# Output norm of three samples and one sample's token scales on ScalarE, four statistics ahead of the branch, half of the last residuals on VectorE

## The chip, the cores and the metric

The kernel runs on one NeuronCore of a Trainium2 chip, in one launch. A core has a matrix engine (TensorE; PE in the profile, PEld for its weight loads), a vector engine (VectorE, DVE), an engine for functions of one operand with a scale and a bias (ScalarE, ACT), a general engine (GpSimd, POOL) and a queue engine that issues transfers (SyncE, SP). Each runs its own instructions in the order in which the program lists them, and waits on semaphores for the others. PE writes to PSUM, which has 8 banks of 128 x 512 numbers; all else lies in SBUF or in HBM. The metric is the device time of one execution in microseconds. Everything is computed in 32-bit floats.

## The reference

Two layers work on x of 16 samples, 256 channels and 64 x 64 pixels (4096 tokens a sample). The first is linear attention with 4 heads of 32, the second a mixture of two out of four convolution experts:

```python
# layer 0
xn  = rmsnorm(gn(x))                       # gn: 32 groups of 8 channels; rmsnorm over channels, per token
q, k, v = split(w_qkv @ xn)                # 3 x 128 rows
q = softmax(q, over the 32 of a head); k = softmax(k, over tokens)
context = k @ v^T                          # per head, 32 x 32
out = w_out @ (context^T @ (q * 32**-0.5)) + b_out
x   = x + rmsnorm(out) * g_out             # rmsnorm over channels, per token
# layer 1
y   = gn(x)
prob = softmax((mean over pixels of y) @ router_w.T / 2); best 2 of 4, weights normalised
for the two experts i of a sample:
    h = gelu(depthwise3x3_i(y) + dw_b_i)
    x = x + weight_i * (pw_i @ h + pw_b_i)
```

## The kernel before

**Tiling.** Channels are the partitions, in two halves of 128 (index k or m). A sample's tokens form 8 groups of 512 (index g) and, for the experts, 4 quarters of 1024 (index j). One sample's x is kept in SBUF in four buffers ("ring") from the first sum to the store, and three samples are under way at once in different phases.

**Phases of a sample.** The names in brackets are functions of the program and tiles of the profile.

1. "in": x is loaded (`load_a`, xa) and BNStats on DVE gathers its statistics (`stats`, st, 16 a sample, one for each g and k; line 264); the `gn0_` functions make a scale and a bias for each channel, with two small PE matmuls (pg, pd). For sample 0 the statistics read the ring directly.
2. "q": x is loaded again (`load_b`, xb); `norm` applies scale and bias (xg, 2 a group: line 305 on DVE for samples below the constant EARLY, line 307 on ACT for the others). PE transposes xg (`turn_x`, px); ACT squares and sums each token (`x_squares`, jx); `token_scale` makes 1/rms (r: a DVE instruction, line 241, and a power on POOL, line 242); `x_keep` writes the scaled tokens (xt, 4 a group: line 331 on DVE below EARLY, line 333 on ACT else). PE projects xg to q and k (`project`, pq); ACT takes the exponential with that scale (`evacuate`, e); PE sums the context over all groups in one bank (`context`, pc); q's softmax follows (`q_sum` on DVE, `q_norm` on POOL, `q_turn` on PE, `q_keep` on ACT). At the end the `mix_` functions fold context, v's weight and the output weight into one matrix (mw).
3. "out": PE applies it (`attend`, po, two halves hf a group); ACT squares and sums (`out_squares`, junk); `out_scale` makes 1/rms (s, DVE and POOL); `out_norm` multiplies (ob: line 463, one DVE instruction of 128 x 512 a half; for the last sample line 461, two ACT instructions of 128 x 256); PE transposes back (`out_turn`, tr); DVE adds to x in the ring (`out_add`, line 477); ACT gathers square sums for the second group norm (`square_sums`).
4. "route": the second norm's scale and bias, the router, the two experts and their weights.
5. "x", by quarters. The depthwise convolution of the first channel half is done on PE: ACT writes a padded copy (`pad0`, pd), SP lays it out in HBM (`lay`) and reads it back spread over partitions (`spread`, xr, 8 a quarter), PE multiplies it by band matrices (`conv0`, dw), ACT applies gelu in place (`gelu0`, line 727). The second half is done on DVE: `pad1` and `start1` on ACT, then 8 taps for each expert (`tap1`, acc, line 741, 128 x 1024), gelu on ACT (`gelu1`, h, line 750). The pointwise matmuls (`pointwise`) collect a quarter in four banks: two parts from h (line 768, weights picked by DVE, lines 591 and 593), two parts from xr with 32-row matmuls (line 779, psp). `residual` adds the bank, the bias and x in one DVE instruction (line 795, 8 a quarter). For the last sample PE adds x by a fifth part, an identity matmul (line 774, 16 records a quarter), and ACT adds the bias only (line 793). `store` writes the result.

**Order.** Every step is a row (phase, sample, group or quarter, name). `place()` gives each row a time: the start of its phase for this sample, plus the slot of the phase times the group, plus the row's own offset from the table PLAN. Rows are sorted by it and issued under a manual schedule, so that this table alone fixes the order on every engine and queue. The unit is a 64th of a sample's period. The first samples and the last have shorter slots for some phases (`in_first`, `q_first`, `out_first` and so on) and shifted starts (`x_0`, `q_1`, `out_e1` and so on; `e1` is the last sample, `e2` the one before).

**Head.** `block_kernel` loads sample 0's x into the ring (16 transfers), then the projection weight; DVE scales the weight (line 1494) and squares it (line 1502), PE sums the columns (pn, line 1505), DVE takes the maximum and compares (lines 1507 and 1508), the result is read into registers (line 1509), and a branch (line 1510) chooses the pipelined path or a general one. The pipelined path's first instructions build small constants on DVE (lines 157 to 174) among the first statistics.

Of the kernel before, what the change touches and what calls it, by code (L numbers as in the profile page):

```python
# [10 lines left out]
FP = mybir.dt.float32  # L11
# [5 lines left out]
P = 128  # L17
# [30 lines left out]
EARLY = 3  # L48
# [5 lines left out]
    "load_x1": 2.47, "mean": 1.04, "means": 4.69, "dev": 5.07, "devs": 8.24, "scale": 8.52,  # L54
# [4 lines left out]
    "evacuate3": 6.83, "context": 7.87, "q_sum": 8.01, "q_norm": 13.4, "q_turn": 15.77,  # L59
    "q_keep": 16.04, "mix_a": 8.41, "mix_turn": 9.67, "mix_v": 10.33, "mix_vv": 11.49, "mix_b": 12,  # L60
    "mix_out": 12.87, "mix_c": 13.33, "mix_lead": 15.68, "attend0": -0.16, "out_sq0": 0.33,
# [3 lines left out]
    "means1": 7.77, "scale1": 8.7, "router": 9.48, "route": 9.99, "choose": 12.08,  # L65
    "pick_taps": 16.41, "route_lead": 22.29, "pick_rows0": 12.27, "pick_rows1": 15.38,
    "pick_row_bias": 13.7, "weigh": 19.29, "pick_bias": 20.19, "pick000": 1.5, "pick100": 11.76,
# [17 lines left out]
    "in_first": 2.74, "in_more": 1.74, "q_first": 9.11, "out_first": 7.86, "out_more": 15.48,  # L85
# [1465 lines left out]
```

## Time and profile before

| | |
|---|---|
| runs | 2724.4 us median of 4 (2722.22 to 2725.16) |
| the profiled execution | 2722.04 us; span 2720.3 us; granted PE clock 0.992 |
| busy: PE, DVE, ACT, POOL | 2635.9 (97%), 2417.5 (89%), 2083.3 (77%), 767.5 us (28%) |
| taps, line 741 (DVE) | 1304.7 us, 1024 of 1284 ns |
| residuals, line 795 (DVE) | 214.5 us, 480 of 475 ns |
| output norm, line 463 (DVE) | 163.6 us, 240 of 682 ns |
| norm, line 307 (ACT) | 169.4 us, 208 of 814 ns |
| token scales, line 333 (ACT) | 168.5 us, 416 of 485 ns |
| identity matmuls, line 774 (PE) | 16.4 us, 64 records |
| moved between HBM and SBUF | 394.77 MB, mean 145 GB/s |

The mean ns of a group are from start to end of one instruction; instructions in a row overlap a little, so that busy time divided by the count is less. The profile has stages with different limits: up to 97 us sample 0 fills the pipeline alone, to 317 us samples 1 and 2 join, to 2425 us all samples look alike, and the last 300 us empty it. The shares over the whole span hide these stages.

### The profile page before, as it was taken

The page shows a single profiled execution, that of the slowest core. Times are in us where ns is not written, and L with a number is a line of the kernel's source. Part 1 is how long each engine was busy: PE and PEld are TensorE (multiplying, and loading weights), DVE is VectorE, ACT ScalarE, POOL GpSimd, SP SyncE. Part 2 cuts the span into 40 slices and gives each one's busy share as a digit, 9 for nine tenths or more (in the row PEclk, how much of TensorE's full clock was granted, in tenths as well). Part 3 has the DMA queues.
Part 4 walks back from the last instruction along what each step waited for, and adds up shares of the span by engine and source line. Part 5 has one row for each costly group of instructions (what it writes and reads, how often), then busy time and mean ns, then how long its engine had stood idle before and what let it go on. Part 6 is the DMA issues. An engine that isn't in the chain of part 4 may idle for free.

```text
span 2720.3 us, 55294 instructions
## 1 busy us (share of the span) xinstructions
PE 2635.9 (97%) x19300; PEld 2257.0 (83%) x19300; DVE 2417.5 (89%) x4480; ACT 2083.3 (77%) x5230; POOL 767.5 (28%) x874
## 2 busy tenths in 40 slices
PE   6898999999999999999999999999999999998888
PEld 5787888888888888888888888888888888886767
DVE  6889998999989898898989989898898988889994
ACT  3576788887887888788787888888788788876643
POOL 2342232322323222232322323233222323232200
PEclk9999999999999999999999999999999999999989
DMA  4335454464545446355354545445454443524332
GB/s 156 113 124 149 140 171 153 133 166 155 155 146 159 156 146 185 128 162 171 126 169 153 156 154 158 155 144 173 142 160 154 145 135 122 149 86 133 122 113 89
DMA packets 229711, 394.77 MB, mean 145 GB/s; under 512 B 25904, under 2 KB 108336, under 8 KB 229424
## 3 DMA queue, kind: packets, MB, share of 16 engines
q1 hardware_dynamic: 228880, 390.75, 46.6%
q8 instruction: 156, 2.56, 0.4%
q14 instruction: 131, 1.07, 0.1%
q10 hardware_dynamic: 544, 0.39, 0.0%
HBM read 280.82 MB, written 110.23 MB: 144 GB/s over the span
## 4 chain that ended last, share of the span: by engine, by line
PE 88%; DVE 7%; ACT 2%; issue 1%; POOL 1%; DMA 1%; ACTq 0%; DVEq 0%; POOLq 0%
PE pw L779 17%; PE pw L768 16%; PE dw L719 15%; PE pq L346 14%; PE pc L364 8%; PE po L440 8%; PE px L315 4%; PE tr L468 4%; DVE acc L741 3%; PE ptq L387 2%; DVE st L264 1%; PE pw L774 1%; DVE ring L795 1%; DVE ring L477 0%; DMA xr<-lay 0%
## 5 line engine op out<-in xcount | busy, mean ns | idle before, releaser
L741 DVE SCALAR_TENSOR_TENSOR acc<-pd,ds,acc 128x1024 f32<-128x1024 f32 x1024 | 1304.7, 1284 | 14.0 <-ACT acc L734 10.2
L242 POOL TENSOR_TENSOR s<-s,mhalf 128x2 f32<-128x2 f32 x256 | 212.3, 831 | 1104.8 <-DVE s L241 1087.0
L346 PE MATMUL pq<-wqkv_n,xg 128*128 128x256 f32 x2048 | 503.9, 384 | 0.9
L719 PE MATMUL dw<-xr,taps 128*128 128x256 f32 x2048 | 489.2, 381 | 8.6 <-ACT xr L727 6.7
L768 PE MATMUL pw<-h,pw 128*128 128x256 f32 x2048 | 481.6, 384 | 15.7 <-ACT h L750 10.0
L779 PE MATMUL pw<-xr,psp 32*128 32x256 f32 x8192 | 484.1, 382 | 0.0
L779 PEld LDWEIGHTS pw<-xr,psp 32*128 32x128 f32 x8192 | 405.3, 185 | 66.2 <-issue 47.2
L768 PEld LDWEIGHTS pw<-h,pw 128*128 128x128 f32 x2048 | 383.0, 192 | 74.8 <-ACT h L750 12.4
L719 PEld LDWEIGHTS dw<-xr,taps 128*128 128x128 f32 x2048 | 374.5, 190 | 59.1 <-ACT xr L727 11.8
L346 PEld LDWEIGHTS pq<-wqkv_n,xg 128*128 128x128 f32 x2048 | 370.2, 191 | 57.8 <-ACT xt L333 11.7
L322 ACT ACTIVATE jx<-px 128x256 f32<-128x256 f32 x512 | 195.4, 382 | 193.5 <-PE px L315 174.4
L354 ACT ACTIVATE e<-pq,r 128x256 f32<-128x256 f32 x512 | 219.7, 470 | 133.8 <-PE pq L346 118.2
L242 POOL TENSOR_TENSOR r<-r,mhalf 128x4 f32<-128x4 f32 x128 | 186.1, 1454 | 448.6 <-DVE r L241 425.3
L795 DVE SCALAR_TENSOR_TENSOR ring<-pw,bs,ring 128x256 f32<-128x256 f32 x480 | 214.5, 475 | 65.7 <-PE pw L768 37.2
L440 PE MATMUL po<-mw,qt 128*128 128x256 f32 x1024 | 253.1, 381 | 0.7 <-DVE ring L795 0.7
L727 ACT ACTIVATE xr<-dw,bv 128x256 f32<-128x256 f32 x512 | 219.5, 478 | 39.7 <-PE dw L719 37.7
L364 PE MATMUL pc<-xt,e 128*128 128x257 f32 x1024 | 245.8, 382 | 3.4 <-DVE xt L331 3.2
L484 ACT ACTIVATE sqj<-ring,nm 128x512 f32<-128x512 f32 x256 | 185.8, 726 | 71.3 <-DVE ring L477 69.5
L477 DVE SCALAR_TENSOR_TENSOR ring<-tr,gout,ring 128x512 f32<-128x512 f32 x256 | 188.8, 746 | 41.5 <-PE tr L468 36.0
L448 ACT ACTIVATE junk<-po 128x256 f32<-128x256 f32 x512 | 196.3, 383 | 27.1 <-PE po L440 22.3
L364 PEld LDWEIGHTS pc<-xt,e 128*128 128x128 f32 x1024 | 189.4, 191 | 29.2 <-issue 2.9
L440 PEld LDWEIGHTS po<-mw,qt 128*128 128x128 f32 x1024 | 190.2, 190 | 28.0 <-issue 2.0
(144 smaller groups left out, 3570.1 us busy)
## 6 DMA issues: line engine op xcount, KB each, us to landing
xr<-lay SPq DMA_DIRECT2D x1024, 66.0 KB
ring<-in_x SPq DMA_DIRECT2D x256, 256.0 KB
out<-ring SPq DMA_DIRECT2D x128, 512.0 KB
xa<-in_x SPq DMA_DIRECT2D x240, 256.0 KB
xb<-in_x SPq DMA_DIRECT2D x240, 256.0 KB
lay<-pd SPq DMA_DIRECT2D x64, 594.0 KB
psp<-layp SPq DMA_DIRECT2D x128, 128.0 KB
layp<-pw SPq DMA_DIRECT2D x16, 256.0 KB
```

What stands on the lines that cost most here:

```text
L242: nc.gpsimd.tensor_tensor(out_t, out_t, mhalf[:, :n], ALU.pow)
L346: nc.tensor.matmul(pq, xg[:, k, c * P : (c + 1) * P], wqkv[:, k, : 2 * HID], start=(k == 0), stop=(k == KH - 1),)
L354: nc.scalar.activation(live["e", b, g][:, c], live["pq", b, g, c // 2][:, c % 2], AF.Exp, scale=live["r", b, g][:, c : c + 1],)
L364: nc.tensor.matmul(live["pc", b], live["e", b, g][:, c, HID:], xt[g % 2][:, c], start=(g == 0 and c == 0), stop=(g == NG - 1 and c == CG - 1),
L440: nc.tensor.matmul(po[:, c], qt[:, n * P : (n + 1) * P], live["mw", b], start=True, stop=True)
L448: nc.scalar.activation(junk[:, :C], live["po", b, g, hf][:, c], AF.Square, accum_out=ss[:, c : c + 1])
L719: nc.tensor.matmul(po, live[f"taps{g}", b][:, d * P : (d + 1) * P], rows3[:, :, d : d + W // 2], start=(d == 0), stop=(d == 1),)
L727: nc.scalar.activation(live["xr", b, j, g][:, 0 : GT // 2], po, AF.Gelu, bias=live["bv", b][:, g : g + 1])
L741: nc.vector.scalar_tensor_tensor(acc, pd1[j % 2][:, t // 3 : t // 3 + QR, t % 3 : t % 3 + W], live["ds", b][:, i, t : t + 1], acc, ALU.mul ...
L768: nc.tensor.matmul(po[q], live["pw1", b][:, part, ms], h[:, q % 2, q // 2], start=begin, stop=end,)
L779: nc.tensor.matmul(po[q], live["psp", b][band, g, ms], live["xr", b, j, g][band, 0 : GT // 2], start=begin and g % 4 == 0, stop=end and g ...
L795: nc.vector.scalar_tensor_tensor(xo, po, bs, xo, ALU.add, ALU.add)
```

## The change

It has five parts. EARLY goes from 3 to 2, so that sample 2's 16 norms and 32 token scales are done by ACT instead of DVE. `out_norm` of samples 0 and 1 is done by ACT, as that of the last sample was already: 64 more ACT instructions of 128 x 256, and 32 fewer on DVE of 128 x 512. Four statistics of sample 0 (groups 0 and 1) are issued in the head, ahead of the branch, into a tile of the head's pool (`st_0`); the other statistics tiles have one buffer instead of two. In the last sample, only quarters 0 and 1 add x by identity matmuls; for quarters 2 and 3 `residual` on DVE adds bank, bias and x, and 32 PE records fall away. And the order: every offset of PLAN has a new value, the depthwise steps of the second channel half (`pad1`, `start1`, `tap1`, `gelu1`) form a phase of their own, "v", and the last sample has its own slots for "x" (15.66 instead of 16) and "v" (15.52), with a shift of the start of "v" (0.34).

```diff
-EARLY = 3
+EARLY = 2
+HEAD_STATS = 2
 PLAN = {
-    "load_x1": 2.47, "mean": 1.04, "means": 4.69, "dev": 5.07, "devs": 8.24, "scale": 8.52,
+    "load_x1": 4.91, "mean": 0.71, "means": 2.85, "dev": 3.38, "devs": 7.33, "scale": 7.4,
...
-    "evacuate3": 6.83, "context": 7.87, "q_sum": 8.01, "q_norm": 13.4, "q_turn": 15.77,
+    "evacuate3": 6.7, "context": 9.31, "q_sum": 9.23, "q_norm": 11.69, "q_turn": 15.93,
...
+    "in_e1": 0.05, "in_e2": 0.12, "pw04": 19.61, "pw14": 23.04, "x_last": 15.66, "v_last": 15.52,
+    "v_e1": 0.34,
 }
...
+    live["st", 0] = st_0
     def stats(b, g, k):
-        st = live["st", b] if ("st", b) in live else new(small, [P, KH, NG, 6], "st", b, bufs=2)
+        st = live["st", b] if ("st", b) in live else new(small, [P, KH, NG, 6], "st", b, bufs=1)
...
-        if b == NB - 1:
+        if b in (0, 1, NB - 1):
             for c in range(2):
                 nc.scalar.activation(ob[:, c], po[:, c], AF.Copy, scale=s[:, c : c + 1])
...
-        n = 5 if b == NB - 1 else 4
+        n = 5 if by_pe(b, j) else 4
...
+    def by_pe(b, j):
+        return b == NB - 1 and j < NQ // 2
...
-        if b == NB - 1:
+        if by_pe(b, j):
             nc.scalar.activation(xo, po, AF.Identity, bias=bs)
...
-                at("in", b, g, f"stats{k}", stats, b, g, k)
+                if b or g >= HEAD_STATS:
+                    at("in", b, g, f"stats{k}", stats, b, g, k)
...
-            at("x", b, j, "pad1", pad1, b, j)
+            at("v", b, j, "pad1", pad1, b, j)
             for i in range(TOPK):
-                at("x", b, j, f"start{i}", start1, b, j, i)
+                at("v", b, j, f"start{i}", start1, b, j, i)
                 for t in range(1, 9):
-                    at("x", b, j, f"tap{i}{t}", tap1, b, j, i, t)
-                at("x", b, j, f"gelu1{i}", gelu1, b, j, i)
+                    at("v", b, j, f"tap{i}{t}", tap1, b, j, i, t)
+                at("v", b, j, f"gelu1{i}", gelu1, b, j, i)
...
-                for part in range(5 if b == NB - 1 else 4):
+                for part in range(5 if by_pe(b, j) else 4):
...
-            "out": turn[0], "route": SLOT, "x": 2 * SLOT,
+            "out": turn[0], "route": SLOT, "x": 2 * SLOT, "v": 2 * SLOT,
         }
-        start = {"x": PERIOD * b}
+        if b == NB - 1:
+            slot |= {"x": PLAN["x_last"], "v": PLAN["v_last"]}
+        start = {"x": PERIOD * b, "v": PERIOD * b}
...
+    st_0 = head.tile([P, KH, NG, 6], FP, name="st_0")
...
         nc.vector.tensor_tensor(sq, wqkv[:, :, : 2 * HID], wqkv[:, :, : 2 * HID], ALU.mult)
+        for g in range(HEAD_STATS):
+            for k in range(KH):
+                nc.vector.bn_stats(st_0[:, k, g], ring[g // 2][:, k, g % 2])
```

More of the change, by code (lines that the diff above doesn't have):

```diff
@@ L53, with pipelined_path @@
 PLAN = {
-    "load_x1": 2.47, "mean": 1.04, "means": 4.69, "dev": 5.07, "devs": 8.24, "scale": 8.52,
[4 rows of a table removed]
-    "evacuate3": 6.83, "context": 7.87, "q_sum": 8.01, "q_norm": 13.4, "q_turn": 15.77,
-    "q_keep": 16.04, "mix_a": 8.41, "mix_turn": 9.67, "mix_v": 10.33, "mix_vv": 11.49, "mix_b": 12,
-    "mix_out": 12.87, "mix_c": 13.33, "mix_lead": 15.68, "attend0": -0.16, "out_sq0": 0.33,
[3 rows of a table removed]
-    "means1": 7.77, "scale1": 8.7, "router": 9.48, "route": 9.99, "choose": 12.08,
-    "pick_taps": 16.41, "route_lead": 22.29, "pick_rows0": 12.27, "pick_rows1": 15.38,
-    "pick_row_bias": 13.7, "weigh": 19.29, "pick_bias": 20.19, "pick000": 1.5, "pick100": 11.76,
[17 rows of a table removed]
-    "in_first": 2.74, "in_more": 1.74, "q_first": 9.11, "out_first": 7.86, "out_more": 15.48,
[12 rows of a table removed]
+    "load_x1": 4.91, "mean": 0.71, "means": 2.85, "dev": 3.38, "devs": 7.33, "scale": 7.4,
[4 rows of a table added]
+    "evacuate3": 6.7, "context": 9.31, "q_sum": 9.23, "q_norm": 11.69, "q_turn": 15.93,
+    "q_keep": 16.06, "mix_a": 10.35, "mix_turn": 11.12, "mix_v": 11.38, "mix_vv": 11.77,
+    "mix_b": 12.09, "mix_out": 13.34, "mix_c": 13.4, "mix_lead": 15.68, "attend0": 0.19,
[5 rows of a table added]
+    "pick_row_bias": 13.88, "weigh": 18.75, "pick_bias": 19.18, "pick000": 1.16, "pick100": 11.36,
[17 rows of a table added]
+    "in_first": 2.73, "in_more": 1.58, "q_first": 9.08, "out_first": 18.07, "out_more": 12.28,
[13 rows of a table added]
 }
 @with_exitstack
-def pipelined_path(ctx, tc, ring, wqkv, x, w_outT, b_out, g_out, router_wT, router_b, dw, dw_b, pwT, pw_b, out):
+def pipelined_path(ctx, tc, ring, st_0, wqkv, x, w_outT, b_out, g_out, router_wT, router_b, dw, dw_b, pwT, pw_b, out):
     nc = tc.nc
@@ L908, in pipelined_path @@
         for phase in start if near else ():
-            start[phase] += PLAN[f"{phase}_{near}"]
+            start[phase] += PLAN[f"{phase}_{near}"] if phase != "v" or near == "e1" else 0
         starts[b], slots[b] = start, slot
@@ L913, in place @@
         phase, b, g, key = row[:4]
-        pace = 1 if phase in ("route", "x") else slots[b][phase] / SLOT
+        pace = 1 if phase in ("route", "x", "v") else slots[b][phase] / SLOT
         return starts[b][phase] + slots[b][phase] * g + PLAN[key] * pace
@@ L1510, in block_kernel @@
     with tc.If(small_logits > 0) as branch:
-        pipelined_path(tc, ring, wqkv, x, *weights_and_out)
+        pipelined_path(tc, ring, st_0, wqkv, x, *weights_and_out)
     with branch.Else():
```

73 rows, old and new, of the table PLAN are left out of this document.

## The prediction

> **What bounds the kernel now.** I read the whole span first as a table of stretches, cut where the stage changes (columns: stretch and its length, then busy time of PE, PEld, DVE, ACT, POOL, granted PE clock, DMA share, GB/s).
>
> ```profile
> 0.00:97.00 97.00, 63.25 (x310) 51.68 (x310) 68.06 (x181) 34.16 (x108) 25.00 (x43) 0.96 0.41 135
> 97.00:174.00 77.00, 76.58 (x438) 68.15 (x437) 66.26 (x173) 58.96 (x203) 30.25 (x35) 1.00 0.38 127
> 174.00:317.00 143.00, 129.66 (x838) 109.70 (x837) 136.96 (x278) 98.46 (x265) 44.57 (x51) 0.95 0.50 148
> 317.00:479.00 162.00, 161.92 (x1203) 139.63 (x1202) 147.27 (x272) 133.87 (x333) 46.99 (x53) 1.00 0.50 155
> ...
> 2425.00:2617.00 192.00, 164.21 (x1308) 132.24 (x1307) 179.80 (x313) 111.73 (x253) 48.12 (x53) 0.96 0.40 117
> 2617.00:2712.00 95.00, 94.53 (x797) 79.81 (x798) 60.40 (x49) 40.79 (x78) 2.06 (x5) 0.99 0.28 99
> ```
>
> To be seen: from 317 to 2425 us every sample takes 162 us with PE busy 161.9 of them, and the waits of PE list nothing between 317 and 2400. There only less PE work helps. At 97 to 174 (B) PE is the bound too. At 174 to 317 (C, the q phase of sample 2) PE has 13 us idle and DVE 6: DVE bounds. At 2425 to 2617 (D) DVE bounds again, 180 of 192; after 2617 (E) PE does, to the end. The first 97 us (A) are a chain of short steps.
>
> Second, the prices, from the groups by form (busy time over the count is what one costs in a row; the last number before the second bar is the latency of one).
>
> ```profile
> L307 ACT ACTIVATE xg<-xb,bi,sc 128x512 f32<-128x512 f32 x208 | 169.4, 814 | 0.0
> L333 ACT ACTIVATE xt<-px,r 128x256 f32<-128x256 f32 x416 | 168.5, 485 | 25.6 <-POOL r L242 22.6
> L463 DVE TENSOR_TENSOR ob<-po,s 128x512 f32<-128x512 f32 x240 | 163.6, 682 | 4.5 <-POOL s L242 4.4
> L331 DVE TENSOR_SCALAR xt<-px,r 128x256 f32<-128x256 f32 x96 | 40.3, 476 | 4.8 <-POOL r L242 4.2
> L305 DVE TENSOR_SCALAR xg<-xb,sc,bi 128x512 f32<-128x512 f32 x32 | 18.0, 564 | 0.0
> L461 ACT ACTIVATE ob<-po,s 128x256 f32<-128x256 f32 x32 | 13.5, 479 | 6.3 <-POOL s L242 6.2
> ```
>
> So on DVE a norm is 0.56, a token scale 0.42, an output norm 0.68 us; on ACT 0.81, 0.405 and 2 x 0.42 us. Third, the chain of work that ended last, in its last 20 us: PE without a break, then the last sample's residuals on ACT.
>
> ```profile
> 2686.12 2.01 PE pw L774 x8
> 2688.12 6.91 PE dw L719 x32
> 2695.03 7.12 PE pw L779 x128
> 2702.15 5.38 PE pw L768 x24
> 2707.53 1.81 PE pw L774 x8
> 2709.33 1.73 PE pw L768 x8
> 2711.06 0.47 PE pw L774 x2
> ```
>
> **The change, part by part.**
>
> *Head statistics.* In the instruction order of DVE four of the 16 BNStats of sample 0 now stand before the branch: two before the weight scale, one before the squares, one before the maximum. In the chain the 12 to 16 statistics after the branch run from 11.34 on at 0.60 each, with 0.65 us of constant-making between them; the four earlier ones sit in DVE's idle time (loads until 6.2, PE's column sums 7.8 to 9.9), except one, which holds the squares, and so the branch, for 0.6. The constants move behind the aggregate, into a wait on PE. 4 x 0.60 - 0.6 + 0.65 = 2.4 off the first PE transpose at 26.1; a late second chunk of x could hold the weight scale instead. I take -2 (0 to -2.4).
>
> *Stage A.* The order of PE now puts half of the next group's x transposes ahead of each context matmul of sample 0. In the chain at 40 to 60 us a group of 7.3 us is: squares, token scale (POOL 1.01), q norm (POOL 1.03), q transposes 0.65, context 1.74, x transposes 0.45, squares again. With the transposes ahead of context, their 0.45 leaves the loop in 7 groups, while the wait on POOL is unchanged: -2.5 (0, if the squares wait on POOL anyway, to -3.1).
>
> *Stage B.* 16 output norms of sample 0 and 4 of sample 2's norms leave DVE (66.3 - 10.9 - 2.3 = 53.1) and come to ACT: 58.96 + 32 x 0.42 + 4 x 0.81 = 75.7 of 77. PE, with 76.6, remains the bound: 0. The cover is gone, though: queued behind the output norm on ACT are squares, exponentials and gelus that PE reads, with 1.3 us of slack in 77. Bounds 0 and +5 (the idle time that DVE shows in C when it is the bound, 6.0).
>
> *Stage C.* DVE loses 12 norms, 32 token scales, 16 output norms of sample 1: 6.8 + 13.4 + 10.9 = 31.1, so 136.96 becomes 105.8. ACT gets 12 x 0.814 + 32 x 0.405 + 32 x 0.422 = 36.2, so 98.46 becomes 134.7. PE needs at most 129.7 (some of it at a granted clock below 1: its mean here is 0.95, and 0.75 in the 20 us around its longest gap at 207). ACT is the next bound: 143 - 134.7 = 8.3, and a little less latency for back-to-back instructions. I take -9; the ends are -13 (PE's own 129.7) and 0 (ACT idles as DVE does, 6, and 2 more for shorter runs). I lie near the busy sum because ACT's inputs here (x by DMA, px and po by PE) are made well ahead.
>
> [...]
>
> *Steady state.* From sample 3 to 14 no instruction changes; the order does. In PE's order the changes between 128-row and 32-row matmuls (the psp ones) fall from 298 to 256; 34 of the 42 lie outside D. The timeline prices one: attend x4 starts at 2392.26 and its successor 0.86 later; the same four between psp blocks take 1.06 to the next start, with two boundaries in it, so 0.10 each. -3 (-1 to -4). The time between a producer and its reader, read off PE's order, does not shrink where it is short: projection to context 1.3 us before, 3.0 after; attend to output transpose 8.9 to 10.2; q phase projection to q transposes 19.5 to 20.4; depthwise to psp 12.7 in both. Hence no new wait is in the sum. SP's transfers keep their shape (loads of x for the sum ahead of each lay-out, the spread ones behind it), and SP stands 644.7 us in 64 waits for the padding that it lays out, some 10 us ahead each time: nothing. POOL is busy 47 of 162 us: nothing.
>
> *Stage D.* In DVE's order one tap and two residuals fewer lie between sample 15's last softmax sum and its last weight pick: 1.19 + 2 x 0.40 = 2.0. DVE idles 9.5 there, for residuals that wait on PE above all; that may close up or widen. -2 (+4 to -9).
>
> *Stage E.* The identity matmuls of quarters 2 and 3 go: 2.01 + 2.01 + 1.81 + 1.81 = 7.6 of PE, which runs here from the last pick to the last sum with 3 to 5 us of waits. Their residuals go to DVE, 16 x 0.40, beside 48 taps of 1.19: 63 of about 87 us; the last drain is 8 x 0.40 instead of 8 x 0.41. The input that PE needs next from DVE, the second expert of quarter 3, has its taps and the residuals done some 6 us before its pointwise matmul by this reckoning. -7.6 (-4 if half of that slack is mispriced, to -8).
>
> Sum: -2 - 2.5 + 0 - 9 - 3 - 2 - 7.6 = -26.1. The profiled execution took 2722.04 (span 2720.3) and becomes 2695.9; the median of the runs, 2724.4, stands 2.4 above it, so 2698.
>
> **The rivals.**
>
> *R1, slower: a wait that recurs in the steady state.* All offsets of the order are new. If one reader on PE, the same in each quarter, stands ahead of its input (the tail shows the price for the second expert's gelu before the pointwise matmul: 10.0 us in 4 waits on L750), it pays once in each of the 52 quarters from sample 2's experts to sample 14's. 26.1 / 52 = 0.50 us a quarter cancels the gain; above that the change is slower. At 0.65 us: 52 x 0.65 = 34, 2698 + 34 = 2732. For it: of a sample's 162 us PE has 0.08 free, so whatever comes late costs in full. Against: the distances above, and ACT with 28 and DVE with 15 us free.
>
> *R2: ACT takes the bound over.* B and C then pay for ACT at 98% and 94%: C's gain is gone, the rest stays: 2698 + 9 = 2707. For it: two of ACT's three new jobs cost more there. Decides from about 8 us of ACT idle in C.
>
> *R3: the tail closes up.* DVE's 9.5 us of waits in D vanish as well, and C reaches PE's limit: 2698 - 7 - 4 = 2687.
>
> *R4: the change does nothing measurable.* R1 at 0.5 us a quarter; 2724.
>
> **How the numbers follow.** Forecast (2690 to 2704) 0.55; R2 (2704 to 2714) 0.18; R3 (2682 to 2690) 0.09; R1 0.15; R4 0.03. The likeliest gives 2698. R1 and R4, 0.18, are left out above, R3's extreme below: 2684 to 2716. A measurement of this kernel tells apart about 0.2%, 5.4 us. Faster: 0.55 + 0.18 + 0.09 = 0.82; same 0.03; slower 0.15.
>
> **What would show it.** Right: the first transpose near 24; C (sample 2's q phase) near 134 with ACT over 95% busy and DVE near 106; 162 us a sample, less 0.2, with no wait of PE; PE in E 7 to 8 us shorter, no L774 in the last 40 us, residuals of the last quarters on L803 (DVE). Wrong: a wait of PE at equal distances from 317 on, ACT below 90% in C with DVE not the bound, or PE waiting in E for the second expert's gelu behind DVE's taps.

## The result, and the profile after

The changed kernel takes 2725.4 us (median of 32 runs, 2722.14 to 2732.6) against 2723.75 us for the kernel before (52 runs): a ratio of 1.0008, 95% interval 1.0003 to 1.0013. That is no change by the 0.2% that I called measurable, where 26 us less had been forecast. The runs scatter more than those of before (10 us against 5.5). The profiled execution took 2729.38 us, 4 above the median; span 2727.6, granted clock 0.989.

The stretches of the changed kernel, cut where those of before were cut (columns: stretch and its length, busy time of PE, PEld, DVE, ACT, POOL, granted PE clock, DMA share, GB/s):

```profile
0.00:97.00 97.00, 68.43 (x320) 56.27 (x321) 69.89 (x185) 35.39 (x115) 27.70 (x45) 0.93 0.42 139
97.00:174.00 77.00, 76.47 (x434) 67.26 (x433) 53.29 (x149) 71.35 (x233) 28.89 (x33) 1.00 0.36 120
174.00:317.00 143.00, 130.57 (x849) 110.90 (x848) 113.69 (x224) 130.23 (x345) 50.23 (x53) 0.96 0.46 145
317.00:479.00 162.00, 159.82 (x1190) 138.01 (x1190) 147.27 (x266) 132.87 (x333) 50.14 (x50) 1.00 0.47 155
...
2425.00:2617.00 192.00, 173.80 (x1348) 142.53 (x1347) 181.74 (x316) 116.45 (x265) 57.80 (x56) 0.95 0.36 117
2617.00:2712.00 95.00, 88.02 (x743) 72.19 (x746) 73.77 (x73) 43.00 (x79) 2.05 (x5) 0.95 0.37 115
```

The work moved: in stage C DVE fell from 137.0 to 113.7 and ACT rose from 98.5 to 130.2 (the prediction's sum had 105.8 and 134.7). PE did hardly more in it: 130.6 instead of 129.7 of 143 us. And from 317 us on PE is no longer busy all the time. The costliest groups of the moved work, by form, show that the prices held:

```profile
L311 ACT ACTIVATE xg<-xb,bi,sc 128x512 f32<-128x512 f32 x224 | 182.7, 816 | 0.0
L337 ACT ACTIVATE xt<-px,r 128x256 f32<-128x256 f32 x448 | 177.3, 481 | 15.8 <-POOL r L244 14.2
L465 ACT ACTIVATE ob<-po,s 128x256 f32<-128x256 f32 x96 | 40.2, 489 | 22.1 <-POOL s L244 22.1
```

Each costs what it cost before (0.82, 0.40, 0.42 us). So the price of an instruction was not the error. The waits of PE from 317 to 2300 us are a part of it; the kernel before lists none here:

```profile
PE tr L472 <- DVE ring L803: 9.6, 12, 1.5
PE pw L783 <- DMA psp<-layp: 2.6, 5, 1.2
PE dw L723 <- DMA xr<-lay: 2.2, 4, 0.7
```

Three new waits: the output transpose on a residual, 0.8 us once in each sample; and, irregularly, matmuls on transfers. At the end (from 2425 us) transfers cost more: `dw` waits for xr 9.2 us in 10, where the kernel before lists 0.9 us in 1. The last 30 us of the chain show such a wait, then the part that went as forecast, no identity matmul (L778) and the last residuals on DVE:

```profile
2697.58 5.19 DMA xr<-lay
2702.77 0.14 issue
2702.91 2.83 PE dw L723 x12
2705.74 7.12 PE pw L783 x128
2712.86 5.82 PE pw L772 x26
...
2718.70 1.37 DVE ring L803 x4
```

To compare stage by stage without the shift of the cuts I took landmarks from the timeline of PE: its first x transpose, each sample's matmul with the output weight (its "mix", L429 before, L433 after, of the "q" phase's end), the last sample's router sums (L527, L531), and PE's last matmul. The time between them, in us, for the profiled executions, with the experiments that the next section explains:

| stretch | before | after | old_order | old_parts | lead2 |
|---|---|---|---|---|---|
| to the first x transpose | 26.1 | 23.9 | 23.8 | 26.6 | 23.9 |
| to sample 0's mix (A) | 71.0 | 69.8 | 71.1 | 68.4 | 68.3 |
| to sample 1's mix (B) | 76.2 | 78.2 | 76.6 | 84.0 | 78.2 |
| to sample 2's mix (C) | 143.5 | 141.9 | 143.8 | 148.6 | 142.0 |
| to sample 15's mix (13 samples) | 2108.2 | 2122.9 | 2109.5 | 2118.1 | 2113.0 |
| to sample 15's router sums (D) | 140.4 | 143.2 | 139.6 | 146.2 | 144.9 |
| to PE's end (E) | 147.5 | 140.1 | 144.5 | 143.9 | 136.5 |
| D and E together | 287.9 | 283.3 | 284.0 | 290.1 | 281.4 |
| to the end of the span | 7.4 | 7.6 | 7.5 | 7.5 | 7.7 |

One landmark does not hold still. Up to sample 15's mix each stretch has the same number of PE records in all these kernels (302 in A, 432 in B, 838 in C, 15614 in the 13 samples). From that mix to the last router sums there are 1006 before and in old_order, but 1078 in the other three: the new table issues the router sums 72 records later. So D is longer and E shorter by that work, about 5 us, whatever is gained, and only their sum compares the two orders.

The change gains 2.2, 1.2 and 1.6 us in the first transpose, A and C, and 4.6 in D and E together. It gives back 14.7 us in the steady state and 2.0 in B.

### The profile page after: what moved, and what is told of

Same layout as the page of the kernel before. It is cut to its first block, busy times and chain, and to the rows that moved or that the text cites. A ratio compares the mean times of both kernels' runs of the same rounds, so it can differ in the third digit from the quotient of the medians.

```text
span 2727.6 us, 55307 instructions
## 1 busy us (share of the span) xinstructions
PE 2637.3 (97%) x19268; PEld 2265.0 (83%) x19268; DVE 2405.4 (88%) x4416; ACT 2129.3 (78%) x5326; POOL 829.5 (30%) x874
## 4 chain that ended last, share of the span: by engine, by line
PE 79%; DVE 11%; DMA 5%; ACT 2%; issue 1%; POOL 1%; SPq 1%; DVEq 0%; ACTq 0%; POOLq 0%
PE pw L783 14%; PE dw L723 14%; PE pq L350 14%; PE pw L772 13%; PE pc L368 7%; PE po L444 7%; DVE acc L745 5%; PE tr L472 4%; PE px L319 4%; DMA xr<-lay 2%; PE ptq L391 2%; DMA psp<-layp 1%; DVE ring L803 1%; DMA xa<-in_x 1%; SPq L692 1%
## 5 line engine op out<-in xcount | busy, mean ns | idle before, releaser
L745 DVE SCALAR_TENSOR_TENSOR acc<-pd,ds,acc 128x1024 f32<-128x1024 f32 x1024 | 1316.0, 1293 | 16.0 <-ACT acc L738 10.5
L244 POOL TENSOR_TENSOR s<-s,mhalf 128x2 f32<-128x2 f32 x256 | 274.0, 1071 | 1208.9 <-DVE s L243 1119.3
L350 PE MATMUL pq<-wqkv_n,xg 128*128 128x256 f32 x2048 | 487.0, 383 | 0.1
L350 PEld LDWEIGHTS pq<-wqkv_n,xg 128*128 128x128 f32 x2048 | 376.6, 191 | 56.7 <-issue 5.6
L803 DVE SCALAR_TENSOR_TENSOR ring<-pw,bs,ring 128x256 f32<-128x256 f32 x496 | 225.5, 475 | 90.5 <-PE pw L772 54.4
L731 ACT ACTIVATE xr<-dw,bv 128x256 f32<-128x256 f32 x512 | 225.3, 479 | 55.0 <-PE dw L723 48.8
L444 PE MATMUL po<-mw,qt 128*128 128x256 f32 x1024 | 244.7, 381 | 0.9 <-DVE mw L436 0.5
```

What stands on the lines that cost most here:

```text
L244: nc.gpsimd.tensor_tensor(out_t, out_t, mhalf[:, :n], ALU.pow)
L350: nc.tensor.matmul(pq, xg[:, k, c * P : (c + 1) * P], wqkv[:, k, : 2 * HID], start=(k == 0), stop=(k == KH - 1),)
L444: nc.tensor.matmul(po[:, c], qt[:, n * P : (n + 1) * P], live["mw", b], start=True, stop=True)
L731: nc.scalar.activation(live["xr", b, j, g][:, 0 : GT // 2], po, AF.Gelu, bias=live["bv", b][:, g : g + 1])
L745: nc.vector.scalar_tensor_tensor(acc, pd1[j % 2][:, t // 3 : t // 3 + QR, t % 3 : t % 3 + W], live["ds", b][:, i, t : t + 1], acc, ALU.mul ...
L803: nc.vector.scalar_tensor_tensor(xo, po, bs, xo, ALU.add, ALU.add)
```

## The experiments

Three theories stood against each other. *Order*: the parts gain, and the new table of offsets loses it. *Parts*: the moved work gains nothing, since DVE was no bound where it was moved. *Transfers*: the loss comes from SP's queue alone. They do not exclude each other; the runs were to give each its share. All medians below stand beside runs of the kernel before on the same chip; lead_tr, no_taps, lead_early3 and lead_norm1 ran on another chip than the rest.

**old_order: the parts without the new order.**

```diff
 PLAN = {
-    "load_x1": 4.91, "mean": 0.71, ...           # all offsets
+    "load_x1": 2.47, "mean": 1.04, ...           # those of before; x_last, v_last 16
-            start[phase] += PLAN[f"{phase}_{near}"] if phase != "v" or near == "e1" else 0
+            start[phase] += PLAN[f"{phase}_{near}".replace("v_", "x_")]
```

> All five code parts of the change with the table of offsets of before (last sample's slots 16, its second-half steps shifted with the first half's). Theory 'the new order costs what the parts gain': a sample takes 162.2 us again from 317 us on (163.4 in the changed kernel's profile), PE has no waits there, the head and the last experts keep their gain (2 and 7.6 us), so 2710 to 2715, 9 to 14 us under before. Rival 'the parts themselves gain nothing, since DVE was no bound in sample 2's q phase and ACT only takes its place': the identity matmuls alone show, 2716 to 2720, with the wait of PE's output transposes around 205 to 215 us as long as before (about 9 us).

Measured: 2719.55 us against 2723.82 (0.9984, 0.9975 to 0.9993). (Five offsets, `x_keep1`, `project2`, `mix_lead`, `q_less` and `stats0`, have the same value in both tables.) The steady state is back at 162.2 us a sample without the waits, as the theory of the order has it, but the gain is 4 us and not 9 to 14: the rival's number. C is 143.8, not shorter at all, though the two parts that leave DVE are in it, and E gained 3.0 of the 7.6 us (D and E together 3.9). Both theories are right in part.

**old_parts: the new order without the parts.**

```diff
-EARLY = 2
-HEAD_STATS = 2
+EARLY = 3
+HEAD_STATS = 0
-        if b in (0, 1, NB - 1):
+        if b == NB - 1:
-        return b == NB - 1 and j < NQ // 2
+        return b == NB - 1
```

(with places for the identity matmuls, 20.4 and 22.0, since the new table has none in the last quarter.)

> The new table of offsets with the code parts undone: norm and token scales of sample 2 on DVE, output norm of samples 0 and 1 on DVE, no statistics in the head, identity matmuls in all quarters of the last sample. Theory 'the new order costs 1.0 to 1.3 us a sample': 2733 to 2745, with the same waits of PE from 317 us on (output transposes behind a residual, 0.8 a sample; matmuls that wait for transfers). Rival 'these waits come from the moved parts': 2720 to 2726, and none of them from 317 on.

Measured: 2745.04 us (1.0078, 1.0065 to 1.0092), and the wait on the residual is there too (10.4 us in 13). The 13 samples take 9.9 us more than before, of the 14.7 of the changed kernel: a loss in the steady state comes with the order and without the parts. The table above adds what I had not expected: in this order the parts are worth 2.7 us in the head, 5.8 in B, 6.7 in C and 6.8 in D and E together, though A and the 13 samples take 1.4 and 4.8 longer with them; by the medians about 20 in all, in the old order 4. The new table suits the moved work and loses without it.

**sp_back: only the transfers' offsets set back.**

```diff
-  "load_x1": 4.91, "load_a0": -13.96, "load_a1": -9.27, "load_b0": -14.48, "load_b1": -11.45,
-  "lay": 7.04, "spread0": 9.04, ... "lay_pw": 9.11, "spread_pw": 15.89, "store0": 32.01, ...
+  "load_x1": 2.47, "load_a0": -16.2, "load_a1": -8.65, "load_b0": -17.65, "load_b1": -7.1,
+  "lay": 4.37, "spread0": 6.43, ... "lay_pw": 10.27, "spread_pw": 12.95, "store0": 29.36, ...
```

> The changed kernel with only the offsets of transfers set back (loads of x, lay-out, spread, picked pointwise weights, stores). Theory 'SP has lost its lead, so the depthwise and psp matmuls wait for transfers': PE's waits on transfers fall from 14.2 us to under 4, the samples of irregular length (up to 165.4) go back to 162.5, 2713 to 2719. Rival 'the transfers' waits are a by-product, and something later would bind': within 2 us of the changed kernel, 2723 to 2727.

Measured: 2719.38 us (0.9983, 0.9974 to 0.9992), some 6 us under the changed kernel. PE's waits on transfers fell from 14.2 to 2.2 us, as the theory has it. The 13 samples take 2113.1 us: of the changed kernel's 14.7 us there, 9.8 were the transfers' offsets and 4.9 belong to the other new ones. From sample 3's mix to sample 14's every sample takes 162.5 us; the irregular ones are gone, and the only waits of PE left from 317 us on are these:

```profile
PE tr L472 <- DVE ring L803: 10.4, 13, 1.5
PE ptq L391 <- ACT e L358: 0.6, 1, 0.6
```

What had happened to SP is seen in its own waits. First the kernel before, then the changed one:

```profile
SPq L681 <- ACT pd L659: 644.7, 64, 18.8
...
SPq L688 <- DMA lay<-pd: 111.2, 64, 3.4
...
SPq L257 <- DVE st L264: 70.0, 33, 15.5
```

```profile
SPq L259 <- DVE st L268: 290.1, 87, 15.6
SPq L685 <- ACT pd L663: 234.1, 50, 15.5
...
SPq L692 <- DMA lay<-pd: 183.3, 62, 4.4
```

SP's time at the lay-out is its lead over ACT: 645 us before, 234 after, and in 14 of 64 quarters none at all. The lead went into waits for buffers of the loads, above all of those that DVE's statistics free (70 to 290 us); the second load of x waits more for ACT's steps (jx and xg, 163 to 285 us), and the ring's load for a store (85 to 193 us). The lay-out, the spread and the weights stand behind those loads in one queue and come late now and then. Set back, SP stands 585.5 us at the lay-out. Which of the 18 offsets matters most was not separated. sp_back also shows a loss of its own, in the last steps of its chain:

```profile
2704.41 1.36 DVE ring L803 x3
2705.77 0.02 issue
2705.79 3.49 DMA out<-ring
```

The last residuals wait 3.5 us for a store that the old offset puts ahead of them.

**lead2: that store's offset left new.**

```diff
-                at("x", b, j, f"store{m}", store, b, j, m)
+                at("x", b, j, f"{end}store{m}", store, b, j, m)   # end_store0 32.01, end_store1 36.98
```

> sp_back once more, but the last sample's last quarter keeps the changed kernel's offsets of its two stores (32.01 and 36.98), so that the first half's store no longer stands ahead of the second half's residuals. (In lead_tr, no_taps, lead_early3 and lead_norm1 the stores of all quarters had kept them, and with loads set back some loads of x came ahead of the store of the sample that held the buffer: their stored output is not the result there, while the work is the same.) Theory 'the residuals wait for that store': the 3.5 us wait in the last 12 us goes, 2715 to 2717. Rival 'the last residuals are bound by DVE': 2719 as sp_back.

Measured: 2716.26 us (0.9972, 0.996 to 0.9983): the 3 us of the theory. This version beats both kernels, the one before by 8 us. It is the base of what follows, but for route_back, lead_tr and the four kernels of stage C: no_start is built on sp_back; lead_tr and the other three set back all of sp_back's offsets but those of the stores.

**Where the 0.75 us of each sample come from: route_back, lead_tr, pw_early, row_late.**

The timeline of sp_back around one such wait, PE and then DVE, with most of the routing arithmetic left out:

```profile
1472.37 3.74 PE L783 MATMUL pw<-xr,psp 32*128 32x256 f32 x64
1476.03 0.66 PE L472 MATMUL tr<-ident,ob 128*128 128x128 f32 x4
1477.43 0.66 PE L472 MATMUL tr<-ident,ob 128*128 128x128 f32 x4 [0.74 <-DVE ring L803]
```

```profile
1472.24 0.16 DVE L535 TENSOR_TENSOR z<-pz,rb 128x4 f32<-128x4 f32 x1
...
1476.56 0.42 DVE L609 TENSOR_REDUCE wv<-wt 128x64 f32<-128x256 f32 x1
1476.90 0.48 DVE L803 SCALAR_TENSOR_TENSOR ring<-pw,bs,ring 128x256 f32<-128x256 f32 x1
```

The quarter's last psp matmul ends at 1476.1. The residual that frees its bank starts 0.8 later, behind 17 small routing instructions, and the second transpose takes that bank. Four edits tried to part the two.

```diff
 # route_back (on the changed kernel)
-  "router": 9.97, "route": 12.08, "choose": 13.85, "pick_rows0": 14.36, "pick_row_bias": 13.88
+  "router": 9.48, "route": 9.99, "choose": 12.08, "pick_rows0": 12.27, "pick_row_bias": 13.7
 # lead_tr (transfers set back, except the stores): a sample's second transpose, its sum and square sum later
+        late = 1.5 if phase == "out" and g == 0 and key in ("out_turn1", "out_add1", "sq_sums1") else 0
 # pw_early (on lead2)
-  "pw11": 22.05, "pw12": 22.36, "pw13": 22.52, "residual10": 24.3
+  "pw11": 20.95, "pw12": 21.26, "pw13": 21.42, "residual10": 23.4
 # row_late (on lead2)
-  "pick_row_bias": 13.88, "pick_rows0": 14.36
+  "pick_row_bias": 14.56, "pick_rows0": 14.6
```

> The changed kernel with only five offsets of the routing step set back (router, route, choose, first row picks, row bias). Theory 'the routing arithmetic on DVE now stands ahead of a residual whose bank the output transpose needs, once a sample': the wait of the transposes on the residual (10.4 us in 13) goes, 0.8 us for each of 13 samples, 2714 to 2717. Rival 'PE only runs ahead elsewhere and the wait moves to another reader': 2723 to 2727 with a new wait of like size.

> The changed kernel with the offsets of loads, lay-out, spread and weight transfers of before (the stores keep their new offsets, unlike in sp_back, where a store issued before the last residuals held them for 3.5 us), and the second output transpose of each sample's first group, with its sum and its square sum, 1.5 units later, behind four more projection matmuls. Theory 'two separate losses of 0.25 and 0.8 us a sample': no wait of a transpose on a residual from 317 us on, a sample takes 161.7 us instead of sp_back's 162.5, and 2705 to 2709. Rival 'the wait moves to the next reader of a bank': a sample stays at 162.4 to 162.6 and 2714 to 2718.

> lead2 with the last three pointwise parts of each quarter's second half 1.1 units earlier (20.95, 21.26, 21.42), so that PE does a transpose of x and the router sums between the psp matmuls and the output transposes, and the first residual of that half 0.9 earlier (23.4), ahead of the routing arithmetic on DVE. Theory 'the transpose waits for a bank that a residual frees, and that residual stands behind 5 us of routing arithmetic': no such wait from 317 us on, a sample takes 161.7 to 161.9 us instead of 162.5, 2705 to 2709. Rival 'as in lead_tr, the wait moves to whoever takes the bank next': a sample stays at 162.4 to 162.6, 2714 to 2718.

> lead2 with two offsets of the routing step later (row bias 14.56, first row picks 14.6), so that on DVE the second half's first residual of a quarter comes ahead of the last 1.6 us of the routing arithmetic; nothing moves on PE. Theory 'each sample PE waits 0.75 us for the bank that this residual frees, because the arithmetic is ahead of it': the wait falls to 0.1 to 0.3 us, a sample takes 161.8 to 162.0 us, 2706 to 2711. Rival 'DVE has no slack there, another wait of like size appears': 162.4 to 162.6 a sample, 2714 to 2718.

Measured: route_back 2727.24 us (1.0009, 1.0 to 1.0018), the wait as long as before (9.0 us in 12), behind a tap and other small instructions instead. lead_tr 2715.01 (0.997, 0.9959 to 0.9982), a sample 162.4: the four projection matmuls now wait for the bank (10.3 us in 13). (In lead_tr, and in three kernels below, some loads of x overtake a store, so that what is stored there is not the result; the expectation of lead2 says so. The work is the same.) pw_early 2821.95 (1.0362, 1.0348 to 1.0376), 170.6 us a sample: a token scale on DVE now waits up to 4.9 us (81 us in all from 641 to 2263) for squares whose x transpose has come behind the psp matmuls; the residual, the routing and the sums behind it are late by as much, and PE loses 8 us a sample. row_late 2726.62 (1.0012, 1.0003 to 1.0021), 163.5 a sample. The wait on the residual was gone, and others stood in its place:

```profile
PE tr L473 <- DVE ob L468: 13.8, 12, 1.2
PE pq L351 <- DVE ring L482: 2.7, 12, 0.2
```

The theory that a reordering of a few rows removes the wait fell in all four: in two the wait stayed at the rival's size, in pw_early and row_late it grew beyond what either side had said. What they share is seen in lead2's stretches from 20 us after a mix on (mix at 1289.0):

```profile
1309.00:1319.00 10.00, 9.25 (x93) 7.52 (x92) 9.48 (x31) 5.37 (x14) 2.99 (x3) 1.00 0.42 139
...
1329.00:1339.00 10.00, 10.00 (x52) 8.86 (x51) 9.97 (x16) 9.56 (x24) 6.22 (x7) 1.00 0.47 158
1339.00:1349.00 10.00, 10.00 (x100) 8.50 (x99) 9.96 (x17) 8.22 (x23) 2.33 (x3) 1.00 0.39 120
```

DVE is full here, 39 of 40 us; from 1302.5 to 1349.9 its idle gaps above 0.1 us add up to 0.19. DVE's 15 us of free time a sample lie nearly all in the rest of the sample. Within this stretch a DVE step that goes ahead, or a wait that DVE gets, makes what stands behind it late by as much, and PE has no slack to take it. So, as I read these rows, the wait moves and does not go. A full DVE is not enough for it: the kernel before has DVE busy 38.3 of the same 40 us, and PE waits for nothing there. It takes the new order as well. Whether an order exists that is free of the wait with the psp blocks of the new table stays open; the old table had one.

**Stage C: no_taps, no_start, lead_early3, lead_norm1.** In finer stretches, the kernel before:

```profile
190.00:200.00 10.00, 7.42 (x33) 5.97 (x34) 9.62 (x31) 6.31 (x21) 6.30 (x10) 0.83 0.34 110
200.00:210.00 10.00, 6.66 (x37) 5.68 (x35) 9.96 (x17) 9.62 (x29) 0.90 (x2) 1.00 0.44 139
210.00:220.00 10.00, 4.47 (x14) 3.52 (x15) 10.00 (x16) 1.72 (x4) 3.86 (x5) 0.50 0.38 118
...
230.00:317.00 87.00, 86.95 (x628) 73.80 (x629) 83.61 (x147) 63.47 (x164) 24.04 (x24) 1.00 0.56 160
```

and the changed one:

```profile
190.00:200.00 10.00, 7.88 (x38) 6.17 (x38) 6.67 (x23) 9.64 (x29) 4.45 (x6) 1.00 0.45 152
200.00:210.00 10.00, 4.39 (x25) 3.32 (x24) 10.00 (x14) 9.37 (x27) 2.66 (x4) 0.89 0.39 139
210.00:220.00 10.00, 6.96 (x24) 5.49 (x24) 9.97 (x18) 7.72 (x22) 5.72 (x5) 0.59 0.33 106
...
230.00:317.00 87.00, 86.90 (x635) 75.50 (x634) 68.21 (x118) 77.72 (x200) 25.81 (x26) 1.00 0.49 152
```

Stage C never was DVE-bound as a whole. From 230 to 317 PE is the bound, 86.95 of 87 us, before the change too. Of PE's 13.3 us of idle time in C, 11.5 lie in the 30 us from 190 to 220, and from 200 to 220 DVE is as full after the change (19.97 of 20) as before (19.96): the relief fell mostly where it was of no use. Four kernels tested what holds PE in these 30 us.

```diff
 # no_taps: sample 0's first quarter without its taps
-                for t in range(1, 9):
+                for t in range(1, 9) if b or j else ():
 # no_start: this, and without that quarter's large padding instructions on ACT
+            if (b, j) == (0, 0) and n > 1:
+                return
...
-        nc.scalar.activation(
+        if b or j:
+          nc.scalar.activation(
 # lead_early3
-EARLY = 2
+EARLY = 3
 # lead_norm1
-        if b in (0, 1, NB - 1):
+        if b in (0, NB - 1):
```

> The changed kernel with the offsets of loads and spread of before; the 16 taps of sample 0's first quarter on DVE are left out (its second channel half is then not convolved there). They are 19 us of DVE work, much of it between 198 and 222 us, where the output norm's small DVE step stands behind them. Theory 'PE waits there because DVE has no time': the waits of the output transposes on ob (9.5 us) go and the stretch from sample 1's mix to sample 2's shrinks from 141.9 to 132 to 135. Rival 'the stretch is set by how early sample 0's experts can start, with PE short of other work': 139 to 142, with the idle time of PE moved in front of the first depthwise matmul.

> sp_back without the 16 taps of sample 0's first quarter (DVE, 19 us) and without its large padding instructions (ACT, some 4 us); that quarter's result is then not the reference's. no_taps alone took 2.8 us off the stretch between the mixes of samples 1 and 2 (141.9 to 139.1) and left the waits of the output transposes at 6.4 of 9.5 us. Theory 'ACT and DVE are both full there with the start of sample 0's experts': 132 to 136. Rival 'the output loop's own steps (PE, ACT, DVE, POOL, ACT, PE in turn) are too long for the order, whatever lies beside': 138 to 140 and the waits stay above 5 us.

> The changed kernel with the offsets of loads and spread of before and the constant EARLY back at 3: sample 2's norms and token scales on DVE. By the prediction's sum (DVE 105.8 + 20.2 = 126 of PE's 130) the stretch from sample 1's mix to sample 2's stays within 1 us of 141.9; by the rival 'each DVE step moved off the 20 us around 205 shortens the wait there' it grows by 2 to 6.

> The changed kernel with the offsets of loads and spread of before and sample 1's output norm on DVE. By the stage sum (DVE 105.8 + 10.9 = 117) the stretch from sample 1's mix to sample 2's stays within 1 us of 141.9; by the rival 'the output norm stands in the wait itself, and DVE is full from 198 to 218' it grows by 1 to 4, with the waits of the transposes on DVE's ob above 9.5.

Measured, in one run each (no_taps 2711.19 us, no_start 2718.42): with 19 us of DVE work gone C takes 139.1 us instead of 141.9. With the padding gone too it takes 136.6, between the theory's range and the rival's, but B 80.1 instead of 77.8, so that both together are no better than no_taps (216.6 and 216.8, sp_back 219.7). The waits of the output transposes on ob shrink and stay: 9.5 us in sp_back, 6.4 in no_taps, 5.5 in no_start. So DVE's taps made a third of them; more than half stays with taps and padding gone, which speaks for the second rival, that the output loop's own steps are too long for the order. The chain of no_start at this place shows that loop:

```profile
199.52 0.63 ACT sqj L488
200.15 0.19 ACT sqj L488
200.33 0.96 ACT xt L337 x3
201.31 0.48 ACT xt L337
201.79 0.73 ACT e L358 x2
202.52 0.70 ACT sqj L488 x2
203.22 0.73 ACT e L358 x2
203.95 0.38 ACT junk L452 x2
```

The output transposes of sample 1 give DVE a sum, whose square sums (sqj) ACT waits for; behind them stand sample 2's token scales and exponentials; only then come the squares (junk) of the next group, then 1/rms on DVE and POOL, ob on ACT, and the next transposes at 208.3. PE had been done with that group's attention at 202. As read from this chain, then, ACT's order closes a loop of some 12 us around PE (transposes at 195.8 and at 208.3), and a part of what the change moves from DVE to ACT (the token scales) lies in it. That the order of these rows, changed alone, shortens C was not tried, so that what holds PE there is in part argued.

lead_early3: C 142.9 (lead2: 142.0), 2716.81 us in one run, as the prediction's sum has it: EARLY is worth 0.9 us in C and nothing measurable in the time. lead_norm1: C 145.9, 2718.57 in one run, transposes waiting 11.7 us for DVE's ob: its rival came true. Kernels with the same stage C (sp_back, lead2, pw_early, row_late, ident_all, last_back, head0) agree in it within 0.2 us. Of the two parts, sample 1's output norm on ACT is worth about 3.8 us in C with the new order (2.5 at PE's end); in the old order both together were worth nothing there.

**The end: ident_all, last_back. The head: head0.**

```diff
 # ident_all (on lead2; places 20.4 and 22.0 for the last quarter's)
-        return b == NB - 1 and j < NQ // 2
+        return b == NB - 1
 # last_back (on lead2): slots and shifts of the last two samples of before
-  "x_last": 15.66, "v_last": 15.52, "v_e1": 0.34, "x_e1": -0.52, "route_e1": 1.73, ...
+  "x_last": 16, "v_last": 16, "v_e1": -0.24, "x_e1": -0.24, "route_e1": 0.66, ...
 # head0 (on lead2)
-HEAD_STATS = 2
+HEAD_STATS = 0
```

> lead2 with the identity matmuls and ACT's residuals in all four quarters of the last sample, as before. By the prediction's term the stretch from the last router sums to PE's end, 136.5 us in lead2, grows by 7.6 to 144, and the time to 2724. Rival 'PE comes to the last quarters sooner and waits there for the spread transfers, so that part of the 7.6 is no gain' (old_order, with this part alone different in that stretch, gained 3.0): it grows by 3 to 5, 2719 to 2721.

> lead2 with the last two samples' shifts and slots of before (16 instead of 15.66 and 15.52, and the e1 and e2 shifts). In sp_back the stretch from the last mix to the last router sums took 144.4 us where the kernel before took 140.4. Theory 'the last sample's own slots lose 4 us there': 140 to 141. Rival 'the loss is that of the new offsets in general': 143.5 to 145.

> lead2 with no statistics ahead of the branch. By the prediction's term the first x transpose comes 2.0 to 2.4 us later than lead2's 23.9 and so does the end; rival 'the time is made up while the pipeline fills': the first transpose comes 2 later, the mix of sample 2 less than 1 later.

Measured: ident_all 2721.41 us (0.9992, 0.9983 to 1.0002), 5 more than lead2, with E at 141.9 instead of 136.5. The waits of PE from 2610 us on, lead2 and then ident_all:

```profile
PE pw L773 <- DVE pw L598: 3.8, 1, 3.8
PE dw L724 <- DMA xr<-lay: 1.6, 4, 0.8
```

```profile
PE pw L773 <- DVE pw L598: 3.2, 1, 3.2
PE dw L724 <- DMA xr<-lay: 0.8, 1, 0.8
```

So 5.3 of the 7.6 us are gained. PE's busy time in E falls by 7.5 (129.1 to 121.6), as priced; the rest goes into waits. In these rows the waits on DVE's last pick and on the last quarters' spread account for 1.4 of the missing 2.3 (5.4 against 4.0), and over all of E, with earlier transfers and a residual's bank, for 2.2: PE comes there sooner than they do. last_back took 2724.74 us in one run, 8.5 more than lead2: D 148.8 instead of 144.9, E 137.9 instead of 136.5, and 165.1 instead of 161.5 for the last sample's step to its mix. With the new offsets the last two samples' own slots and shifts gain; the theory that they lose was wrong. The loss in D that it set out to explain is the moved landmark: in route_back, with the routing offsets of before, 1006 PE records stand in D again, which takes 139.5 us, E takes 142.9, and the two together 282.4, against 287.9 before. head0 took 2718.90 in one run; its first transpose comes at 26.6 instead of 23.9, sample 2's mix 2.7 later and PE's end 2.8 later. The head's gain reaches the end in full here (in old_order 1.4 of it was lost in sample 3).

## Why the prediction was wrong

The forecast was 2698 us, the range 2684 to 2716, faster at 0.82; measured were 2725.4. It is the case of R4 that came true, by a mechanism near that of R1: a wait once in each sample, where R1 has one in each quarter, and late transfers, which no rival has, eat the gain. R1 and R4 had 0.18 between them.

- *Head* (-2): right. -2.2 to the first transpose; 2.7 by head0, a little more than its bound of 2.4.
- *Stage A* (-2.5): right in size with the transfers set back (-2.7 in lead2), half of it lost in the changed kernel (-1.2). Without the new order A gains nothing (71.1 in old_order). That the x transposes are what left the loop was not tested.
- *Stage B* (0, ends 0 and +5): +2.0, inside the bounds. The waits that PE lists there are 0.5 us for DVE's mw, just behind sample 0's mix, and 0.4 for ACT's exponentials, so that the cover on ACT, which was named, is at most a part of it.
- *Stage C* (-9): the step that failed first. -1.6 came. "DVE bounds" was read from one row over 143 us; cut finer, the same trace had PE at 86.95 of 87 in the last 87 us and 11.5 of its 13.3 us of idle time in 30 us, in the last 20 of which DVE stays full. As far as the runs show, the output loop's dependent steps and sample 0's taps hold PE there; what closes the loop is read from one chain and stays open. R2, that ACT takes the bound over, gave the right size for a reason that does not show: ACT was busy 130 of 143 us, idle 13 where R2 names 8.
- *Steady state* (-3): +14.7 in the profiled execution, 9.8 by the offsets of the transfers and 4.9 by the rest of the order. This is the largest miss, and three sentences failed in it. "Hence no new wait is in the sum": I had compared producers and readers by their distance in PE's order, and never when another engine frees the bank that a PE step takes; the residual on DVE behind the routing arithmetic is such a step, 0.8 us a sample. "DVE with 15 us free" is the average of a sample with a full stretch of nearly 50 us (the kernel before has one of some 40 us too). And "SP ... some 10 us ahead each time: nothing" took a lead of 645 us for safe without asking what stands ahead of the lay-out in the new order: the loads now stand waiting for DVE's statistics and the lead shrank to 234, with transfers late irregularly. The offsets that I had before me (spread 9.04 instead of 6.43 before a matmul at 11.34 instead of 10.64; the weights' spread 15.89 instead of 12.95 before one at 18.58 instead of 18.17) said that these transfers had lost about half of their time ahead. The gain that I did forecast is there: less its wait, a sample of lead2 takes 162.5 - 0.8 = 161.7 us, 0.5 less than before, where fewer 32-row blocks were to bring 3 / 13 = 0.2. That it comes from these blocks was not tested apart.
- *Stages D and E* (-2 and -7.6): together -4.6 by the table; that E alone comes to -7.4 there is luck, made by the moved landmark. The prediction cut them at DVE's last weight pick, a landmark that the new order leaves in place (799 PE records follow it before, 795 in ident_all). Cut there, D is 1.6 us shorter in the changed kernel and 0.3 in lead2: the -2 holds in the one and not in the other. E is 3.0 shorter, and 6.2 in lead2. The term of the identity matmuls had the work right and took the waits behind it for unchanged: by ident_all they bring 5.3 of 7.6, and the waits on the pick and the spread grow, since PE comes to them sooner. The rest of the miss in the changed kernel goes with the late transfers again, 9.2 us of waits on xr after 2425 us, 2.4 in lead2.

By the prices both norms cost more on ACT (the norm 0.81 against 0.56 us, the output norm 2 x 0.42 against 0.68). lead_early3, which moves norm and token scales back to DVE together, gained nothing: 2716.81 against 2716.26 us, C 0.9 longer. For the output norm, sample 1's alone, ACT was the better place in the new order by 3.8 us in C, although the rows price it higher there; the reason, as far as the waits show it, is DVE's queue, not the price: in lead_norm1 the output transposes wait 11.7 us in 4 for DVE's ob, in lead2 8.6 in 3 for ACT's.

## What to carry to other kernels

Cut a stage until an engine that you call its bound is full in each piece, and ask where exactly the engine that matters is idle: work taken from a full engine counts only in those microseconds. When an order is rewritten, follow the queue engine and the buffers too: for each transfer what stands ahead of it in its queue and waits, and for each PSUM bank which engine frees it and what that engine does just before. A lead or a free time given as an average over a sample protects nothing; the shortest one counts, and to move a wait is not to remove it. Before you compare stretches between landmarks, count the work between them: a landmark that the change itself moves turns one stretch's gain into another's loss.

## What was not expected of the hardware

Late transfers came irregularly: samples of the same order took between 162.5 and 165.4 us in one execution, and the changed kernel's 32 runs spread over 10.5 us, where those of sp_back spread over 2.7 (2718.16 to 2720.88, 11 runs). Around PE's longest idle time in C, 5.4 us up to 212.0 before the change and 4.8 up to 209.8 after, the granted clock was low: in 210 to 220 us it was 0.50 before and 0.59 after, and the first projection matmuls then started 427 ns apart instead of 216; in the changed kernel the seven from 215.1 us on cost 1.5 us that way.
